# Two elements' WKV recurrence started earlier in the issue order of a fused Flamingo kernel: the third from the first place of the first grid batch, the fourth from its place 10

## The chip, the cores and the metric

One NeuronCore of one Trainium2 chip runs the whole program in one launch. The metric is the device time of that launch in microseconds (us). The kernel before was timed three times: 1096.87, 1093.98 and 1094.46, median 1094.46. A separate execution was profiled; its span, from the first instruction to the last, is 1092.4 us, and the launch around it took 1094.21.

Five instruction streams work side by side and meet at semaphores: PE (matmuls; its weight loads are listed as PEld), DVE (vector work, scans, reductions), ACT (activations and copies out of PSUM), POOL (a second, slower elementwise engine), and SP (issues the DMA transfers). Each stream runs its instructions in the order in which they were put there.

## What is computed

Four batch elements of 512 rows by 512 features go through two gated blocks, all in float32 at the interface:

```python
x = x + tanh(g_xattn[0]) * WKV(w, u, layernorm(x), ctx)        # a recurrence over the 512 rows
x = x + tanh(g_ffn[0])   * FFN(layernorm(x), w1, w2, w3)       # sign weights, activations rounded by groups of 64
x = x + tanh(g_xattn[1]) * ATT(layernorm(x), ctx, wq, wkv, wp) # 16 heads of 32, all 512 context rows
x = x + tanh(g_ffn[1])   * TERNARY(layernorm(x), gamma, W)     # one 512x512 layer, weights -1, 0, 1
```

The recurrence of the first line, per feature, for each row t with k = layernorm(x) and v = ctx:

```python
no = max(o, u + k);  A = exp(o - no);  E = exp(u + k - no);  y = (A*p + E*v) / (A*q + E)
no2 = max(w + o, k); A2 = exp(w + o - no2); E2 = exp(k - no2)
p, q, o = A2*p + E2*v, A2*q + E2, no2
```

The elements do not depend on each other. Within one element the four lines depend on each other in this order, so the WKV of an element has to be through before its FFN begins.

## The kernel before

**How a WKV is tiled.** `wkv_layer` handles one element. It takes the statistics of the four row tiles of 128 (L191, L194 on DVE), centres each tile (L215 on ACT), turns it on PE (`wk_ps`, four 128x128 transposes for a tile) and copies it out (L584 on ACT), so that features lie on partitions and the 512 rows lie along the free axis. Then come four chunks of 128 features. A chunk is a chain across engines: a scan for the running maximum (L599, DVE), a subtraction (L608, POOL), four activations and two exponentials (L612, L614, ACT), a scan for q (L629, DVE), products (L630 POOL, L632 DVE), a scan for p (L634, DVE), sums and products (L635, L636, L641, L642, POOL), two reciprocals of 256 columns (L640, DVE), the last product (L645, DVE), four transposes back (`wy_ps`, PE) and the gated sum into x (L653, DVE). For the third and fourth element a chunk also loads its v from a scratch tensor in HBM (L594, `wk_v<-cD`, issued by SP). The pool of these tiles has one buffer of each name, so that two chunks overlap only at their ends. The four chunks follow each other eight steps apart (`in_steps(chains, 8)`), 32 steps in all.

**How the order of the work is set.** The stages of all elements are Python generators. Each is registered with `line(...)` and a list of parts `(start, end, steps)`, which give every step a place on one axis; `run` always advances the generator whose next step has the lowest place. The places decide in which order the stages' matmuls stand in PE's queue, because each step's matmuls are tied behind those of the step before. The streams of the other engines are filled from the same sequence, with some reordering by the scheduler of the framework.

The axis: 0 to 0.3 is the start (context keys and values, weights, WKV of the first element). From 0.3 to 0.97 the FFN of the first element runs, 16 units of one row tile and one block of 512 hidden features each (`at_unit(n)` is its unit n). Then come three grid batches, from place b to b + 1 for b = 1, 2, 3. Each has 17 slots (`SLOTS`), and a slot is 1/17. In grid batch b the FFN of element b takes its 16 units, one in a slot, and between them stand the steps of the attention of element b - 1 (from slot 5 on, over 18 slots, so that it reaches slot 6 of the next batch), then the output projection of that element (`project_out`, slots 6 to 8 of the next batch) and its ternary layer (`ternary`). After the third batch the attention of the fourth element runs alone.

**Where the four WKVs stood.** The first element's is in the start. The second's is in the first FFN, its 32 chunk steps from unit 5 to unit 14. The third's and the fourth's were placed by one loop, `for b in (2, 3)`: x is loaded 4.2 slots before place b - 1, the statistics are taken 3.2 slots before it, the four transposing steps are at its slots 1.8 to 5.8, the 32 chunk steps at its slots 5.05 to 13.05. So the first grid batch had the whole WKV of the third element, the second grid batch that of the fourth, and the third grid batch had none.

**Names that the steps below touch.** `ff_hp` and `ff_acc` (L162) are the matmuls of the FFN, `tp_ps` (L165) the transposes between them. A unit's chain from the second `ff_hp` group runs over L750, L222, L676, L678, L680 (DVE), L684 (ACT), L685 (POOL) to `tp_ps`. `s_ps`, `pt_ps`, `o_ps` are the matmuls of the attention, L948 and L950 its maximum and exponential, L970 the copy of the turned scores. `at_o`, `qr_ps` and `p_ps` belong to the output projection; `tf_xn`, `qr_ps` and `f_ps` belong to the ternary layer, whose chain to PE is L219 and L1147 (POOL), L222 to L1159 (DVE), L231 (ACT). L724 loads FFN weights, L913 the attention's keys and queries.

Of the kernel before, what the change touches and what calls it, by code (L numbers as in the profile page):

```python
# [30 lines left out]
def kernel(  # L31
# [518 lines left out]
    def load_batch(b):  # L550
        xb = st.tile([P, NT, D], F32, name=f"xb{b}", tag="xb")
        rows = x[b].rearrange("(t p) d -> p t d", p=P)
        if b:
            nc.sync.dma_start(out=xb, in_=rows)
        else:
            for t in range(NT):
                nc.sync.dma_start(out=xb[:, t, :], in_=rows[:, t, :])
        return xb
# [628 lines left out]
    def next_batch(b):  # L1187
        xs[b] = load_batch(b)
        yield
        yield from wkv_layer(b, xs[b])  # L1190
# [15 lines left out]
    def run(until):  # L1206
        while lines:
            now = min(lines, key=place)
            if place(now) > until:
                return  # L1210
            try:
                next(now["gen"])
                now["step"] += 1
                next_turn()
            except StopIteration:
                lines.remove(now)
# [3 lines left out]
    SLOTS = NT * NF + 1  # L1220

    def line(gen, *parts, aside=False):
        lines.append({"gen": gen, "parts": parts, "step": 0, "aside": aside})

    xs = {}
    with (
# [19 lines left out]
        def at_unit(n):  # L1246
            return 0.3 + 0.67 * n / 16.0
# [84 lines left out]
            (at_unit(16), at_unit(16.4), 7),  # L1332
        )
        line(next_batch(1), (at_unit(0.5), at_unit(0.5), 1), (at_unit(0.6), at_unit(0.6), 1), (at_unit(2.0), at_unit(5.0), 4), (at_unit(5.0), at_unit(14.0), 32))
        for b in (2, 3):
            line(
                next_batch(b),
                (b - 1.0 - 4.2 / SLOTS, b - 1.0 - 4.2 / SLOTS, 1),
                (b - 1.0 - 3.2 / SLOTS, b - 1.0 - 3.2 / SLOTS, 1),
                (b - 1.0 + 1.8 / SLOTS, b - 1.0 + 5.8 / SLOTS, 4),  # L1340
                (b - 1.0 + 5.05 / SLOTS, b - 1.0 + 13.05 / SLOTS, 32),
            )
        run(0.99)
    nc.sync.dma_start(out=gamma_b, in_=bcast(gamma))
    ps = ctx.enter_context(tc.tile_pool(name="ps", bufs=1, space=PSUM))
# [78 lines left out]
```

## Time and profile before

| | us |
|---|---|
| median of three runs | 1094.46 |
| the profiled execution, launch and span | 1094.21, 1092.4 |
| PE busy in the span | 943.3 |
| DVE busy | 827.0 |
| ACT busy | 729.9 |
| POOL busy | 320.7 |

Busy time is summed over one engine's instructions, overlaps counted once. Matmuls have modelled ends, so a PE that is shown busy may still run at half its clock; the profile has a column for the clock that was granted (1.00 is full). The grid batches can be found in the trace by the matmuls of their FFNs: the first `ff_hp` matmul of the second element starts at 329 us, that of the third at 513, that of the fourth at 738, and the third batch's 16 slots are over at about 925. So the three batches took 184, 225 and 187 us.

### The profile page before, as it was taken

To read this page: it belongs to the slowest core of one execution; us is meant where nothing else is said; L and a number is where in the kernel's file an instruction comes from. 1 tells how busy PE (TensorE), PEld (TensorE's weight loads), DVE (VectorE), ACT (ScalarE), POOL (GpSimd) and SP (SyncE) were. 2 spreads that over 40 slices of the span, in tenths; PEclk is the share of its full clock that TensorE was granted. 3 is DMA by queue.
4 is the path that set the end of the run, shared out by engine and by line. 5 is a ranking of instruction groups with operands and counts; after the bars stand their busy time and mean duration, and the time that the engine had idled before them with its cause. 6 is when DMAs were issued, how large, how long until landed. Compare 5 with 4: busy or idle time off the path is not lost.

```text
span 1092.4 us, 17928 instructions
## 1 busy us (share of the span) xinstructions
PE 943.3 (86%) x6350; PEld 680.0 (62%) x6380; DVE 827.0 (76%) x1600; ACT 729.9 (67%) x1490; POOL 320.7 (29%) x328
## 2 busy tenths in 40 slices
PE   3879997998879888799997886999999999878975
PEld 2345564565557666677775665677776777655652
DVE  5985548757876899896769898966687866579976
ACT  5656755567545776667877576677685777877863
POOL 3831104423333254621215545412122410100000
PEclk8889999999999999999999798999999999989998
DMA  8188845464445674645576354655574563244311
GB/s 288 39 272 317 323 169 190 144 221 155 154 146 181 221 234 127 231 129 169 185 234 204 121 177 133 204 195 180 184 231 156 184 210 116 59 148 116 116 42 39
DMA packets 85674, 189.68 MB, mean 174 GB/s; under 512 B 12241, under 2 KB 36817, under 8 KB 74577
## 3 DMA queue, kind: packets, MB, share of 16 engines
q1 hardware_dynamic: 85584, 188.53, 51.7%
q8 instruction: 51, 0.84, 0.3%
q14 instruction: 39, 0.31, 0.1%
HBM read 148.65 MB, written 39.85 MB: 173 GB/s over the span
## 4 chain that ended last, share of the span: by engine, by line
PE 49%; DVE 22%; ACT 14%; POOL 5%; issue 5%; DMA 4%; SPq 1%; ACTq 0%; POOLq 0%; DVEq 0%
PE ff_hp L162 15%; PE pt_ps L165 7%; PE ff_acc L162 6%; PE o_ps L162 4%; PE v_ps L162 4%; PE s_ps L162 3%; ACT at_P L950 3%; DVE wk_q L640 3%; ACT at_PT L970 3%; DVE at_nm L948 2%; PE k_ps L162 2%; DVE wk_p L634 1%; PE qr_ps L165 1%; PE tp_ps L165 1%; ACT wk_e L612 1%
## 5 line engine op out<-in xcount | busy, mean ns | idle before, releaser
L162 PE MATMUL ff_hp<-wT,xp 128*128 128x512 f32 x1024 | 275.7, 412 | 6.6 <-DVE ff_z L746 3.7
L162 PEld LDWEIGHTS ff_hp<-wT,xp 128*128 128x128 f32 x1024 | 195.4, 196 | 54.6 <-DVE ff_z L746 5.7
L950 ACT ACTIVATE at_P<-s_ps,at_nm 128x512 f32<-128x512 f32 x256 | 175.0, 690 | 45.2 <-DVE at_nm L948 43.4
L948 DVE TENSOR_REDUCE at_nm<-s_ps 128x1 f32<-128x512 f32 x256 | 166.6, 677 | 38.4 <-PE s_ps L162 37.9
L970 ACT COPY at_PT<-pt_ps 128x512 f32<-128x512 f32 x224 | 131.2, 590 | 72.6 <-PE pt_ps L165 71.9
L685 POOL TENSOR_TENSOR ff_z<-qg_b,qg_s 128x512 f32<-128x512 bf16 x64 | 71.9, 1124 | 314.6 <-ACT qg_b L684 304.7
L165 PE MATMUL pt_ps<-ident,at_P 128*128 128x128 f32 x1024 | 155.4, 280 | 9.0 <-ACT at_PT L970 4.3
L165 PEld LDWEIGHTS pt_ps<-ident,at_P 128*128 128x128 f32 x1024 | 118.1, 142 | 47.3 <-ACT at_PT L970 10.9
L162 PE MATMUL ff_acc<-wT,hr 128*128 128x512 f32 x512 | 137.6, 409 | 5.2 <-DVE hr L697 2.6
L162 PE MATMUL s_ps<-at_kR,at_qR 128*128 128x512 f32 x256 | 103.0, 464 | 24.0 <-ACT at_P L950 17.6
L162 PEld LDWEIGHTS ff_acc<-wT,hr 128*128 128x128 f32 x512 | 92.9, 191 | 26.2 <-DVE hr L697 4.2
L162 PE MATMUL o_ps<-at_PT,at_V 128*32 128x128 f32 x2048 | 75.4, 281 | 4.7 <-ACT at_PT L970 2.8
L162 PEld LDWEIGHTS o_ps<-at_PT,at_V 128*32 128x32 f32 x2048 | 54.8, 111 | 28.6 <-issue 11.6
L746 DVE SCALAR_TENSOR_TENSOR ff_z<-ff_z,ff_hp 128x512 f32<-128x512 f32 x64 | 43.4, 679 | 37.0 <-ACT ff_z L745 36.9
L745 ACT ACTIVATE ff_z<-ff_hp,coef 128x512 f32<-128x512 f32 x64 | 44.1, 688 | 40.5 <-PE ff_hp L162 38.1
L750 DVE SCALAR_TENSOR_TENSOR ff_z<-ff_hp,coef,ff_z 128x512 f32<-128x512 f32 x64 | 47.7, 745 | 30.2 <-PE ff_hp L162 30.1
L684 ACT CAST qg_b<-qg_i 128x512 bf16<-128x512 int8 x80 | 49.3, 617 | 27.4 <-DVE qg_i L680 17.3
L162 PEld LDWEIGHTS s_ps<-at_kR,at_qR 128*128 128x128 f32 x256 | 43.3, 194 | 36.4 <-ACT at_P L950 25.2
L162 PE MATMUL v_ps<-wkvT,cT 128*128 128x512 f32 x128 | 60.5, 618 | 5.5 <-DVE wT L303 2.3
L162 PE MATMUL k_ps<-cT,wkvT 128*128 128x512 f32 x128 | 61.3, 631 | 2.3 <-ACT wk_k L584 1.0
L640 DVE RECIPROCAL wk_q<-wk_q 128x256 f32<-128x256 f32 x32 | 54.5, 1722 | 3.0 <-POOL wk_q L635 1.6
L696 ACT CAST hr<-tp_ps 128x512 fp32r<-128x512 f32 x64 | 37.6, 588 | 21.7 <-PE tp_ps L165 21.7
(180 smaller groups left out, 1669.4 us busy)
## 6 DMA issues: line engine op xcount, KB each, us to landing
wT<-wD SPq DMA_DIRECT2D x72, 1024.0 KB, 5.4
wn<-in_L_ffn_w_dram SPq DMA_DIRECT2D x18, 1024.0 KB, 6.2
at_kR<-kD SPq DMA_DIRECT2D x128, 128.0 KB, 4.0
at_qR<-qD SPq DMA_DIRECT2D x256, 64.0 KB, 2.5
wD<-wT SPq DMA_DIRECT2D x12, 1024.0 KB, 4.2
kD<-k_half SPq DMA_DIRECT2D x16, 512.0 KB, 2.8
qD<-at_half SPq DMA_DIRECT2D x32, 256.0 KB, 2.2
cn<-in_ctx_dram SPq DMA_DIRECT2D x8, 512.0 KB, 5.9
```

The lines of the kernel that those rows point to most:

```text
L162: return in_turn(nc.tensor.matmul(*args, **kwargs))
L165: return in_turn(nc.tensor.transpose(*args))
L640: nc.vector.reciprocal(half, half)
L684: nc.scalar.copy(qb, qi)
L685: nc.gpsimd.tensor_tensor(grouped(src), grouped(qb), s.unsqueeze(2).to_broadcast([P, NG, GS]), ALU.mult)
L696: nc.scalar.copy(part[:, 0, :], pt)
L745: nc.scalar.activation(z, hp, AF.Tanh, scale=coef[:, 0:1])
L746: nc.vector.scalar_tensor_tensor(z, z, 1.0, hp, ALU.add, ALU.mult)
L750: nc.vector.scalar_tensor_tensor(z, hp, coef[:, 1:2], z, ALU.mult, ALU.mult)
L948: nc.vector.tensor_reduce(nm, sp, AX.X, ALU.max, negate=True)
L950: nc.scalar.activation(lanes[k, i, t], sp, AF.Exp, bias=nm, accum_out=sums[k][:, t, i : i + 1],)
L970: made[k] = nc.scalar.copy(dst, blocks(pt))
```

## The change

The loop over the third and fourth element is replaced by two calls, one for each, with other places. Nothing is computed in another way, and no instruction is added or removed.

```diff
-        for b in (2, 3):
-            line(
-                next_batch(b),
-                (b - 1.0 - 4.2 / SLOTS, b - 1.0 - 4.2 / SLOTS, 1),
-                (b - 1.0 - 3.2 / SLOTS, b - 1.0 - 3.2 / SLOTS, 1),
-                (b - 1.0 + 1.8 / SLOTS, b - 1.0 + 5.8 / SLOTS, 4),
-                (b - 1.0 + 5.05 / SLOTS, b - 1.0 + 13.05 / SLOTS, 32),
-            )
+        line(
+            next_batch(2),
+            (at_unit(12.0), at_unit(12.0), 1),
+            (at_unit(13.6), at_unit(13.6), 1),
+            (at_unit(14.2), at_unit(16.2), 4),
+            (1.0 + 1.0 / SLOTS, 1.0 + 9.8 / SLOTS, 32),
+        )
+        line(
+            next_batch(3),
+            (1.0 + 5.0 / SLOTS, 1.0 + 5.0 / SLOTS, 1),
+            (1.0 + 7.5 / SLOTS, 1.0 + 7.5 / SLOTS, 1),
+            (1.0 + 9.8 / SLOTS, 1.0 + 11.8 / SLOTS, 4),
+            (1.0 + 12.0 / SLOTS, 2.0 + 7.0 / SLOTS, 32),
+        )
```

For the third element the transposing steps move into units 14.2 to 16.2 of the first FFN, and the chunks start at slot 1 of the first grid batch, 2.2 slots for each chunk where there were 2. For the fourth element the statistics move to slot 7.5 of the first grid batch, the transposing steps to slots 9.8 to 11.8, and the four chunks stand at slots 12, 15, 18 and 21 counted from place 1, three slots for each. So two of its chunks are in the first grid batch, and two are in the first seven slots of the second. The WKV of the first and second element stay where they were.

## The prediction

> **What bounds the kernel now.** I read the sums by stretch first: the three grid batches, cut where the first `ff_hp` matmul of each FFN starts in the timeline (329, 513, 738 us) and where the 16 slots of the third are over (925).
>
> ```profile
> 329.00:513.00 184.00, 163.34 (x1087) 126.95 (x1089) 157.15 (x284) 125.50 (x261) 70.94 (x71) 0.96 0.56 182
> 513.00:738.00 225.00, 196.51 (x1437) 151.22 (x1444) 181.49 (x358) 158.89 (x332) 85.96 (x82) 0.95 0.55 183
> 738.00:925.00 187.00, 181.40 (x1392) 141.67 (x1399) 134.36 (x304) 132.52 (x293) 44.02 (x44) 0.99 0.56 179
> ```
>
> Columns: length, then busy time of PE, PEld, DVE, ACT, POOL, the granted clock, DMA share, GB/s. The third batch, without a WKV, is bound by PE (181.4 of 187). The second has the same FFN, attention, projection and ternary work and a WKV on top: 47.1 us more DVE, 15 us more PE, and 38 us more time. The excess is what can be won.
>
> Then the same by sub-stretch, cut at slots 5, 10, 12 of the first batch and slot 7 of the others.
>
> ```profile
> 329.00:376.00 47.00, 42.94 (x204) 32.89 (x205) 33.00 (x61) 27.33 (x50) 11.91 (x13) 0.97 0.62 202
> 376.00:428.00 52.00, 44.34 (x306) 34.51 (x308) 50.97 (x81) 38.89 (x83) 23.95 (x24) 0.97 0.56 182
> 428.00:454.00 26.00, 23.33 (x170) 18.18 (x168) 23.30 (x42) 17.78 (x39) 16.38 (x17) 0.93 0.65 211
> 454.00:513.00 59.00, 52.72 (x413) 41.37 (x411) 49.88 (x106) 41.49 (x92) 18.70 (x17) 0.97 0.47 153
> 513.00:593.00 80.00, 74.33 (x554) 57.58 (x556) 59.86 (x120) 61.20 (x131) 24.02 (x23) 1.00 0.62 210
> 593.00:738.00 145.00, 122.18 (x884) 93.64 (x889) 121.63 (x239) 97.68 (x203) 61.94 (x60) 0.92 0.51 168
> 738.00:810.00 72.00, 70.99 (x540) 55.96 (x543) 53.02 (x120) 53.69 (x119) 14.03 (x15) 1.00 0.60 194
> 810.00:925.00 115.00, 110.41 (x854) 85.71 (x857) 81.34 (x185) 78.84 (x175) 29.99 (x30) 0.99 0.53 170
> ```
>
> Call them A to H. B is DVE-bound (51.0 of 52); A has 14 us of free DVE. F is bound by neither engine and lasts 30 us longer than H, its twin without a WKV; its clock is 0.92. So I asked what PE waited for in F:
>
> ```profile
> PE qr_ps L165 <- ACT tf_xn L231: 8.6, 1, 8.6
> PE qr_ps L165 <- ACT at_o L231: 3.9, 1, 3.9
> PE tp_ps L165 <- DVE at_y L1036: 2.7, 1, 2.7
> PE f_ps L162 <- ACT at_PT L970: 2.2, 1, 2.2
> ```
>
> In H no such wait is above 0.9 us. These are the projection's and ternary layer's chains, arriving late. The chain of waits around the longest of them shows why:
>
> ```profile
> 644.59 1.59 POOL wk_e L630
> 646.18 1.45 POOL ff_z L685
> 647.63 2.17 POOL wk_q L635
> 649.86 1.63 issue
> 651.49 1.70 DVE wk_q L640
> ...
> 663.13 1.52 POOL tf_xn L219 x2
> 664.64 0.50 POOL tf_xn L1147
> ```
>
> WKV work on POOL and DVE stands directly ahead of the rest.
>
> **The change part by part.** No instruction is added; work moves. One chunk costs DVE, from the mean rows of L599, L629, L632, L634, L640 (twice), L645, L653: 1.41 + 1.34 + 1.01 + 1.84 + 3.44 + 0.97 + 0.74 = 10.75 us. Its slowest rows (2.22, 2.23, 1.78, 2.29, 3.50, 1.73, 0.75) give 14.5, the upper bound of a chunk; 3.7 us more. ACT has four 0.72 and two 1.07, 5.0; POOL six operations, 1.42 + 1.56 + 1.44 + 1.7 + 1.36 + 1.29 = 8.8; PE four transposes of 0.27. I take DVE as the measure, because it was full where chunks ran, and B's fullness (0.98) as the pace of a full stretch.
>
> *A, slots 0 to 5.* The third element's chunks now start at slot 1. Out: its early scans, 2.5 us in the timeline. In: two chunks and one scan, 22.9. DVE: 33.0 - 2.5 + 22.9 = 53.4, at 0.98 it is 54.5: +7.5. PE work (43) cannot hide it. Bounds: +6.4 (DVE wholly full) to +14 (two chunks at 14.5). A chunk's own chain is no tighter: the gated sums came at 396.1, 420.2, 446.4 and 473.0 us, 24 to 27 us apart, and A would give 27 for each. PE's order has the first `wy_ps` transposes in slot 3 and the next in slot 5; if a chain is late there, PE stands, with `ff_acc` and the second `ff_hp` queued behind. That is inside the 7.5.
>
> *B, slots 5 to 10.* WKV in B was 22.6 us of DVE; now chunks three and four less the scan, 20.1, and the fourth element's statistics, 4 x 0.85 = 3.4. DVE 51.9, at 0.98 53: +1 (0 to +3).
>
> *C, slots 10 to 12.* A gap. DVE loses 8.3, PE loses one `wy_ps` group and gets the fourth element's 16 `wk_ps` transposes, 16 x 0.32 = 5: 27.2, less the 1.7 that a half-clock stretch in it (0.93) cost. Bound by PE: 0 (0 to +2).
>
> *D, slots 12 on.* Out: 9.3 of WKV and 3.4 of statistics; in: nearly two chunks, 20. DVE 49.9 - 12.7 + 20 = 57.2, PE 52.7 unchanged. At 0.96 for both 59.6, and I take 61, since both are nearly full: +2 (0 to +5.5).
>
> *E, slots 0 to 7 of the second batch.* Out: 11.6 of WKV on DVE, 16 `wk_ps`. In: two chunks and a remainder of 1.7, 23.2. DVE 71.5, PE 74.3 - 5.1 + 3.3 = 72.5. Its twin G lasts 72. Two engines at 0.94 give 77: -3 (-8, G's length, to +4, DVE at 78.8).
>
> *F.* No WKV is left in it: H's 115, and 2 for the remaining disorder: 117, -28. Bounds -30 (H) to -13 (the 17.4 us of waits above stay, and only the rest goes).
>
> *The first FFN's end.* Twelve `wk_ps` transposes and three centrings and copies move into it: 3.8 us of PE, in the stretch from 300 to 329 us, where PE was busy 23.0 of 29. The idle 6 us hide them; where they don't, it is 3.8. I take +1 (0 to 3.8). The x load keeps its place in SP's queue in both built programs.
>
> *SP.* A v load (L594) waits for the chunk before it (L636 on POOL), and what follows in the queue waits with it: now FFN weights (L724) and the first q stores in A, later queries (L913).
>
> ```profile
> SPq L594 <- POOL wk_e L636: 28.2, 6, 8.3
> ```
>
> These were prefetched by a slot or more, so I take +2 (0 to 8, one longest wait uncovered).
>
> Sum: 7.5 + 1 + 0 + 2 - 3 - 28 + 1 + 2 = -17.5. On the profiled span, 1092.4 - 17.5 = 1074.9. The median is 2.06 above that span (1094.46 - 1092.4), so 1077.
>
> **A rule that speaks against it.** DVE's L632 takes 0.68 us at best and 1.78 at worst, with POOL reading at the same time. The Trainium skill, page "SBUF — State Buffer", section "SBUF: two separate sides", says that a DVE operation with two SBUF inputs and a POOL operation that reads SBUF exclude each other for a whole instruction. A holds the attention's POOL work, and now WKV's too. By the rule each of a chunk's five such operations could wait for a POOL operation of 1.27 us, on top of the shortest rows' 9.0: 15.4 for a chunk, and A would be +16 instead of +7.5. The mean rows contain such encounters already, so the sum goes by them.
>
> **The rivals.** (1) *The first batch swallows it.* DVE's free time in A and D takes the chunks, E runs at G's pace: all the low bounds together, 6.4 - 8 - 30 = -31.6, 1063. For: A and D have 14 and 9 us free. Against: a chunk is a serial chain over four engines with single buffers. (2) *Work only changes place.* A chunk costs 9.5 us (38/4) wherever it is; six in the first batch, two in the second: 1094. For: DVE is 0.85 full in the first batch already. Against: slots 5 to 13, first `ff_hp` to first `ff_hp` (366 to 469 us), took 12.9 us each, the two after 480 some 11: 3.8 for a two-slot chunk, far below 9.5. (3) *Slower: the waits in F are the ternary layer's own.* If POOL, DVE and ACT deliver `tf_xn` and `at_o` as late without WKV, the 17.4 us and the half-clock stretches around them stay (598 to 605, 615 to 622, 656 to 667, some 8 us of loss beside the waits): F gains 5, E 3, and 13.5 are paid elsewhere: +5.5, 1100. It decides from F gaining less than 10. For: the operation that ends each wait is the layer's own. Against: H has the same chains without such waits.
>
> **How the numbers follow.** Forecast 0.70, rival 1 0.10, rival 2 0.08, rival 3 0.12. The forecast's own range is 1064 to 1090. A measurement can tell 0.3% from no change (1091.2 to 1097.7). Faster: forecast less 0.01, rival 1 and a quarter of rival 2, 0.81; same: half of rival 2 and 0.02 from the edges of the forecast and rival 3, 0.06; slower 0.13. All high bounds together (1121) are no case; 1063 to 1092 leaves out rival 3, most of rival 2 and a tail below, 0.2.
>
> **What would show it.** The second batch from first `ff_hp` to first `ff_hp` near 197 us, its PE waits on `tf_xn` and `at_o` under 1 us each and the clock near 1.0 after slot 7; the first batch near 194, with DVE above 0.95 in slots 0 to 10; the third at 187. Wrong would be a first batch above 212, `wy_ps` waits in slots 3 and 5 above a few us, or F above 132 us.

## The result

The changed kernel took 1105.77 us in the median of four runs (1102.51 to 1107.30), the kernel before 1094.39 on the same chip (1093.98 to 1096.87). The ratio is 1.0095, its 95% interval 1.0068 to 1.0122. I had forecast 1077 within 1063 to 1092: the sign was wrong. The profiled execution of the changed kernel took 1107.30, its span is 1105.5.

The sums by stretch, cut as before at the first `ff_hp` of each FFN (columns: length, busy time of PE, PEld, DVE, ACT, POOL, granted clock, DMA share, GB/s):

```profile
333.00:540.00 207.00, 172.03 (x1095) 132.19 (x1098) 176.03 (x297) 134.51 (x274) 89.68 (x89) 0.92 0.53 169
540.00:752.00 212.00, 192.53 (x1417) 149.08 (x1424) 166.43 (x346) 146.82 (x313) 69.53 (x66) 0.95 0.54 179
752.00:939.00 187.00, 181.17 (x1400) 141.25 (x1410) 135.34 (x306) 133.90 (x296) 44.02 (x44) 1.00 0.59 192
```

The second batch won 13 us, the first lost 23, the third is as it was, and the first batch starts 4 us later. DVE's sum in the first batch, 176 us, is close to what the prediction's parts add up to (157 + 20); but the stretch lasted 207 us, far longer than that sum. The sub-stretches A to F of the prediction, cut at the same units of the FFN in both kernels (A holds the first six units, so it ends where slot 6 begins; B holds four, C two, D four, E seven, F nine):

```profile
333.00:394.00 61.00, 46.62 (x201) 34.88 (x204) 54.20 (x76) 32.93 (x58) 31.48 (x32) 0.92 0.54 174
394.00:453.00 59.00, 50.22 (x308) 38.09 (x307) 49.48 (x86) 36.12 (x77) 23.81 (x23) 0.86 0.48 154
453.00:475.00 22.00, 21.87 (x178) 17.93 (x177) 20.33 (x53) 18.94 (x42) 8.24 (x10) 1.00 0.65 216
475.00:540.00 65.00, 53.32 (x414) 41.30 (x412) 52.02 (x86) 46.52 (x100) 26.15 (x24) 0.97 0.52 163
540.00:632.00 92.00, 79.03 (x546) 61.16 (x549) 77.82 (x144) 63.96 (x133) 34.84 (x33) 0.91 0.54 181
632.00:752.00 120.00, 113.50 (x873) 87.92 (x876) 88.61 (x203) 82.85 (x181) 34.70 (x34) 0.99 0.54 178
```

| | before | forecast | measured |
|---|---|---|---|
| A, slots 0 to 5 | 47 | 54.5 | 61 |
| B, slots 5 to 10 | 52 | 53 | 59 |
| C, slots 10 to 12 | 26 | 26 | 22 |
| D, slots 12 on | 59 | 61 | 65 |
| E, slots 0 to 7 of the second batch | 80 | 77 | 92 |
| F, the rest of the second batch | 145 | 117 | 120 |

F came nearly as forecast. The reader should look at E: DVE is busy 77.8 of 92 us and PE 79.0, so neither engine is full, and the stretch is still 20 us longer than its twin without a WKV (72). The granted clock is 0.91 in E and 0.86 in B. Lost clock costs PE at most (1 - clock) x length: 8 us in each.

The waits of PE in A, and those in E, say what stood in the way (engine, line, what it waited for: us, times, longest):

```profile
PE wy_ps L165 <- DVE wk_e L645: 4.1, 1, 4.1
PE tp_ps L165 <- POOL ff_z L685: 3.1, 1, 3.1
PE ff_hp L162 <- DVE ff_z L750: 2.5, 1, 2.5
```

```profile
PE qr_ps L165 <- ACT at_o L231: 4.2, 1, 4.2
PE ff_hp L162 <- DVE ff_z L746: 3.5, 1, 3.5
PE s_ps L162 <- ACT at_P L950: 3.1, 2, 2.8
PE ff_hp L162 <- DVE ff_z L750: 2.6, 1, 2.6
```

Two pieces of the timeline show how such a wait comes about (start, length, instruction, in brackets the engine's own idle time before it and what ended it). The first is in A, the second in E, with the ACT instruction that L746 needs:

```profile
352.48 1.43 DVE L632 TENSOR_TENSOR wk_q<-wk_e,wk_q 128x512 f32<-128x512 f32 x1
353.84 1.22 DVE L634 TENSOR_TENSOR_SCAN wk_p<-wk_e 128x512 f32<-128x512 f32 x1
356.16 3.37 DVE L640 RECIPROCAL wk_q<-wk_q 128x256 f32<-128x256 f32 x2 [1.11 <-POOL wk_q L635]
359.44 0.65 DVE L750 SCALAR_TENSOR_TENSOR ff_z<-ff_hp,coef,ff_z 128x512 f32<-128x512 f32 x1
360.10 1.73 DVE L645 TENSOR_TENSOR wk_e<-wk_e,wk_q 128x512 f32<-128x512 f32 x1
```

```profile
565.71 0.69 ACT L745 ACTIVATE ff_z<-ff_hp,coef 128x512 f32<-128x512 f32 x1
568.53 2.27 DVE L634 TENSOR_TENSOR_SCAN wk_p<-wk_e 128x512 f32<-128x512 f32 x1 [1.17 <-POOL wk_e L630]
570.73 0.66 DVE L746 SCALAR_TENSOR_TENSOR ff_z<-ff_z,ff_hp 128x512 f32<-128x512 f32 x1
```

In A, DVE works 7 us for the chunk, 1.1 of it standing idle for POOL, before it takes the 0.65 us of L750 that the FFN's unit needs; PE, whose order has `wy_ps` next, stands 4.1 us until L645 is done: here it waits for the chunk itself. In E it waits for FFN work behind the chunk: L746's input is done at 566.4, but the scan L634 stands before it in DVE's queue, first waits 1.17 us for POOL, then takes 2.27 us, and L746 starts at 570.7: PE's 3.5 us. A queue that runs in order can be the bound without being full.

### The profile page after: what moved, and what is told of

It reads as the page before. It is cut to its first block, busy times and chain, and to the rows that moved or that the text cites. A ratio compares the mean times of both kernels' runs of the same rounds, so it can differ in the third digit from the quotient of the medians.

```text
span 1105.5 us, 17930 instructions
## 1 busy us (share of the span) xinstructions
PE 948.9 (86%) x6350; PEld 683.9 (62%) x6380; DVE 832.4 (75%) x1600; ACT 731.7 (66%) x1490; POOL 322.2 (29%) x328
## 4 chain that ended last, share of the span: by engine, by line
PE 49%; DVE 25%; ACT 12%; POOL 6%; issue 5%; DMA 3%; SPq 0%; POOLq 0%; ACTq 0%; DVEq 0%
PE ff_hp L162 16%; PE pt_ps L165 7%; PE ff_acc L162 6%; PE o_ps L162 4%; PE s_ps L162 3%; PE v_ps L162 3%; ACT at_P L950 3%; PE k_ps L162 3%; DVE wk_q L640 2%; ACT at_PT L970 2%; DVE wk_p L634 2%; DVE at_nm L948 2%; PE qr_ps L165 2%; DVE qg_i L680 2%; DVE ff_z L750 1%
## 5 line engine op out<-in xcount | busy, mean ns | idle before, releaser
L162 PE MATMUL ff_hp<-wT,xp 128*128 128x512 f32 x1024 | 281.9, 419 | 18.4 <-DVE ff_z L746 8.3
L162 PEld LDWEIGHTS ff_hp<-wT,xp 128*128 128x128 f32 x1024 | 198.9, 199 | 70.1 <-DVE ff_z L746 11.7
L685 POOL TENSOR_TENSOR ff_z<-qg_b,qg_s 128x512 f32<-128x512 bf16 x64 | 72.0, 1125 | 318.9 <-ACT qg_b L684 305.4
L750 DVE SCALAR_TENSOR_TENSOR ff_z<-ff_hp,coef,ff_z 128x512 f32<-128x512 f32 x64 | 47.4, 741 | 32.8 <-PE ff_hp L162 32.7
L746 DVE SCALAR_TENSOR_TENSOR ff_z<-ff_z,ff_hp 128x512 f32<-128x512 f32 x64 | 43.4, 679 | 36.7 <-ACT ff_z L745 36.5
L697 DVE TENSOR_TENSOR hr<-tp_ps,hr 128x512 fp32r<-128x512 f32 x64 | 43.7, 682 | 12.1 <-ACT hr L696 12.0
```

The lines of the kernel that those rows point to most:

```text
L162: return in_turn(nc.tensor.matmul(*args, **kwargs))
L685: nc.gpsimd.tensor_tensor(grouped(src), grouped(qb), s.unsqueeze(2).to_broadcast([P, NG, GS]), ALU.mult)
L697: nc.vector.tensor_tensor(part[:, 1, :], pt, part[:, 0, :].bitcast(F32), ALU.subtract)
L746: nc.vector.scalar_tensor_tensor(z, z, 1.0, hp, ALU.add, ALU.mult)
L750: nc.vector.scalar_tensor_tensor(z, hp, coef[:, 1:2], z, ALU.mult, ALU.mult)
```

## The experiments

Each run is set against executions of the kernel before on the same chip (medians 1093.98 to 1095.23); so the prices below are differences of ratios to it, times 1094.4. Stretch lengths are those of each run's own profile, cut at the same units.

**The third element alone** moved, the fourth at its old place (the diff is against the changed kernel, and the fourth's other three times go back in the same way):

```diff
-            (1.0 + 5.0 / SLOTS, 1.0 + 5.0 / SLOTS, 1),
+            (1.0 + 12.8 / SLOTS, 1.0 + 12.8 / SLOTS, 1),
...
```

> The third element's WKV at its new place (turned at the end of the first FFN, chunks from slot 1 to 9.8 of the first grid batch), the fourth's at its old one. Theory A (place): the first five slots, with FFN work alone, are a bad place, because a unit's chain there has only one slot of about 7 us and PE stands behind every late chain; so the first batch keeps most of its loss with four chunks instead of six: about 192 us (184 before, 207 in the changed kernel), the second batch 225 as before, the end of the first FFN +4, together 1104 to 1110. Rival B (number): six chunks in one batch are too much for DVE, four are not; first batch 180 to 186, second 225, together 1092 to 1098.

1098.96, ratio 1.0046 (1.0029 to 1.0064), between the two ranges and 1 us above Rival B's. A is 61 us, so Theory A's loss there is real; but C and D give it back (21 and 51), and the first batch sums to 186, as Rival B said. The kernel loses a few us at the end of the first FFN (its first batch starts at 333 instead of 329). Moving the third element alone makes the kernel 5 us slower; B, without the fourth's statistics, is 53.

**The fourth element alone** moved, behind the third at its old place (the fourth's lines):

```diff
+            (1.0 + 11.0 / SLOTS, 1.0 + 11.0 / SLOTS, 1),
+            (1.0 + 13.3 / SLOTS, 1.0 + 15.3 / SLOTS, 4),
+            (1.0 + 15.0 / SLOTS, 2.0 + 7.0 / SLOTS, 32),
```

> The third element's WKV at its old place (slots 5 to 13), the fourth's behind it: turned at slots 13.3 to 15.3, chunks from slot 15 of the first grid batch to slot 7 of the second, 2.25 slots each. Theory A: slots 0 to 12 of the first batch as before, the gain of 25 us after slot 7 of the second batch is kept, slots 0 to 7 of the second batch pay some 10 us for each of three chunks less what is there now (about 100 us against 80): 1085 to 1093. Rival B: with only one chunk more in the first batch and DVE not full in the second, slots 0 to 7 take no more than 80 and the kernel comes to 1068 to 1078.

1093.35, ratio 0.9986 (0.9972 to 0.9999), just above Theory A's range. F falls from 145 to 120; D rises from 59 to 72 and E from 80 to 90. What F gains, D and E pay. The two moves alone come to +5 and -2 us, both together to +10; but the fourth's places are not the same here and in the changed kernel, so the 7 us between are not shown to be crowding.

**What four chunks cost at each place.** Four runs left out an element's chunks in the kernel before and in the changed one:

```diff
+        if b in (3,):            # (2,) in the runs without the third element's
+            for _ in range(32):
+                yield
+            return
         chains = [chunk(c) for c in range(NC)]
```

> The kernel before with the four chunks of the fourth element's WKV left out (its statistics and transposes stay). It prices these chunks at their old place. Theory A and my forecast agree here: second batch near 190 us instead of 225, 1057 to 1064. Were the waits on the projection's and ternary layer's chains their own (rival 3 of the prediction), the second batch would stay above 205 and the kernel above 1072.

> The changed kernel with the same four chunks left out. Theory A: the first batch keeps a loss of some 10 us in its first ten slots (near 195), slots 0 to 7 of the second batch fall from 92 to 74, that is, two chunks cost about 9 us each there although DVE was busy only 77.8 of 92 us; 1070 to 1078 in all. Rival B (number): with four chunks the first batch falls to 184 or less, and the whole is 1057 to 1064, the same as the kernel before without these chunks. If slots 0 to 7 of the second batch stay above 85, the chunks there are not what made them long.

> The changed kernel with the four chunks of the third element's WKV left out (statistics and transposes stay). Theory P (a chunk has one price of 8 to 10 us, mostly PE waits and the half clock that follows them, wherever it stands): 1065 to 1073, slots 0 to 5 of the first batch near 44 us, slots 5 to 10 near 45. The model of my prediction (a stretch lasts as long as its fullest engine's sum) would give slots 0 to 5 at 44 and slots 5 to 10 at 47, and the whole 1068: the two differ in the next run, not here.

> The kernel before with the same four chunks left out: the price of the third element's chunks at their old place. Theory P: 31 to 39 us less, 1056 to 1064, first batch 146 to 152 us. The model of my prediction: PE-bound without them, 163 us of PE less 4.4 of transposes, that is some 162 with gaps, 22 us less, 1073. Far less than that, or far more, would mean that the place decides the price.

| left out | median, ratio and interval | price of the four chunks |
|---|---|---|
| fourth's, kernel before | 1060.70, 0.9688 (0.9672 to 0.9704) | 34 us |
| fourth's, changed kernel | 1066.07, 0.9738 (0.9721 to 0.9754) | 39 us |
| third's, kernel before | 1065.99, 0.9750 (0.9727 to 0.9773) | 27 us |
| third's, changed kernel | 1069.61, 0.9780 (0.9761 to 0.9798) | 35 us |

The prices are good to 2 or 2.5 us in the kernel before and 3.5 in the changed one. The fourth's chunks cost 34 us at their old place and 39 at the new one. Without them, E and F of the changed kernel are the first two lines here, and E and F of the kernel before the last two:

```profile
525.00:596.00 71.00, 70.24 (x539) 55.12 (x538) 51.72 (x117) 52.49 (x116) 13.73 (x14) 1.00 0.64 212
596.00:714.00 118.00, 112.54 (x876) 86.90 (x875) 89.31 (x210) 84.90 (x187) 34.64 (x34) 1.00 0.59 194
512.00:586.00 74.00, 72.62 (x556) 57.38 (x556) 52.58 (x118) 57.31 (x125) 13.71 (x14) 1.00 0.62 206
586.00:705.00 119.00, 112.81 (x877) 87.00 (x876) 89.26 (x210) 85.18 (x187) 34.63 (x34) 1.00 0.61 194
```

In the changed kernel E is 71 instead of 92 us: the fourth's chunk work in it, 26 us on DVE in the windows, made it 21 us longer in a stretch where DVE had 19 us free. Of the 21 us, 12 are PE standing (13.0 us of E with the chunks, 0.8 without) and 9 are PE busy longer (79.0 against 70.2) with nearly the same matmuls, at a clock of 0.91 instead of 1.00. So in E the price is PE's waits and the clock lost after them. The run as a whole (1066.07) lies between the ranges of Theory A and Rival B; A and B stay at 61 and 59 with four chunks in the first batch, so six were not needed to make them dear. In the kernel before without the fourth's chunks, the second batch takes 193 us instead of 225, and its waits of 8.6 us on `tf_xn` and 3.9 on `at_o` are gone (the longest left is 1.7): rival 3 of the prediction is refuted. The third's 27 us at the old place lie between the 22 of the prediction's model and the 31 that Theory P had as its least; its 35 at the new place are within Theory P's range, where the prediction's model gave the same time.

**Less DVE work in a chunk, or the same in two pieces**, both in the changed kernel:

```diff
             for h in range(2):
                 half = den[:, h * (T // 2) : (h + 1) * (T // 2)]
-                nc.vector.reciprocal(half, half)
+                if b < 2:                                  # first run
+                    nc.vector.reciprocal(half, half)
...
+                nc.vector.reciprocal(half, half)           # second run
+                if b and h == 0:
+                    yield True
```

> The changed kernel without the two reciprocals (3.44 of a chunk's 10.75 us on DVE) in the third and fourth elements' WKV. If the price is DVE time standing ahead of the FFN's and attention's short operations, it falls with it: eight chunks at some 3 us, 1077 to 1087. If the price is the number of links of the chunk's chain, or its work on ACT and POOL, it falls by less than 10 us: 1096 to 1104.

> The changed kernel with a chunk's two reciprocals in two steps instead of one (the spare step before the transposes back is used for it, so the number of steps stays): the same work, but other instructions may stand between the two halves in DVE's queue. If long uninterrupted DVE work is what PE waits for (waits of 2.5 to 4.8 us on ff_z and wk_e), these waits lose up to 1.7 us each and some of the half-clock stretches with them: 5 to 12 us less, 1094 to 1101. If only the sum of DVE work matters: 1103 to 1108.

The first run concerns the third and fourth element, the second the second element too. Without the reciprocals 1094.49, ratio 1.0000 (0.9990 to 1.0010): 27.5 us of DVE work less bring 10 us, between the ranges of the two expectations. In two steps 1096.81, ratio 1.0021 (1.0012 to 1.0030): 8 us for no work less, only some 2 us fewer. So the sum of DVE work is at most a part of what is paid for. The largest waits did not get shorter, though (4.9 and 3.5 us on L746, as in the changed kernel), so the expected mechanism, 1.7 us off each wait, is not what happened; L750 in A now goes between the halves, and B runs at a clock of 0.94 instead of 0.86, A at 0.84 instead of 0.92. Nor was there much to separate: in the changed kernel's trace, DVE already ran other instructions between the two reciprocals in seven of the eight chunks, and only the first chunk's pair stands together (the 3.37 us in A above). The edit also puts the second reciprocal, POOL's L641 and L642 and the last product one step later, so that the transposes back follow the product without a spare step. Which of these brings the 8 us is not shown.

**The statistics out of B:**

```diff
-            (1.0 + 7.5 / SLOTS, 1.0 + 7.5 / SLOTS, 1),
-            (1.0 + 9.8 / SLOTS, 1.0 + 11.8 / SLOTS, 4),
+            (1.0 + 10.4 / SLOTS, 1.0 + 10.4 / SLOTS, 1),
+            (1.0 + 11.0 / SLOTS, 1.0 + 12.4 / SLOTS, 4),
```

> The changed kernel with the fourth element's statistics moved from slot 7.5 to 10.4 of the first batch and its transposes to slots 11 to 12.4. Slots 5 to 10 took 59.0 us with these statistics (3.4 us of DVE) and 52.8 without them in the run with the third element alone. Theory (crowding): in a stretch where DVE is full, 3.4 us more make PE wait a little and then run at half clock (17 us of it there); moved out, slots 5 to 10 fall to about 53 with less than 7 us at half clock, and the kernel to 1098 to 1102. If the statistics are not the cause, the stretch stays above 57 and the kernel within 3 us of the changed one.

B falls to 54 us as expected, but the kernel only to 1103.64, ratio 1.0076 (1.0061 to 1.0091): the other expectation, and not clear of the changed kernel's interval. A, whose program is the same, ran at a clock of 0.81 in this profile and 0.92 in that of the changed kernel:

```profile
331.00:393.00 62.00, 49.97 (x199) 38.26 (x201) 53.46 (x76) 32.23 (x57) 30.87 (x32) 0.81 0.50 166
393.00:447.00 54.00, 46.39 (x307) 35.49 (x307) 47.45 (x77) 35.45 (x76) 22.18 (x21) 0.94 0.51 169
```

A few us of a single stretch may be the clock of that execution. B also came to 53 to 56 us in four runs that leave the statistics where they were (without the reciprocals, with them in two steps, without Relu, without three POOL operations), so its 59 is not shown to be the statistics' doing.

**The split on the kernel before**, the same edit of the reciprocals:

> The kernel before with a chunk's two reciprocals in two steps instead of one. In the changed kernel this took 9 us away. If long uninterrupted DVE work is what makes a chunk dear, it does so at the old places too: 1084 to 1091. If it only mended the crowded slots of the changed kernel: 1092 to 1096.

1085.28, ratio 0.9910 (0.9891 to 0.9929), as the first theory had it: the fastest version with the whole computation, 10 us below the kernel before and 20 below the changed one. Here five of the eight pairs stood together before and one of eight with the edit; but the other moves that come with it are the same as above, so the separation alone is not shown to be the cause. F falls from 145 to 139, B and C by 3 together. In F the waits of 3.9 us on `at_o` and 2.7 on `at_y` are gone; the one on `tf_xn` stays, at 9.0.

**Work taken from a chunk on ACT and on POOL**, in the third and fourth element:

```diff
-                nc.scalar.activation(e[:, i, :], z, AF.Relu, bias=at, scale=sign)
+                if b < 2:        # without Relu: the exponentials read z, with scale 0
+                    nc.scalar.activation(e[:, i, :], z, AF.Relu, bias=at, scale=sign)
...
-            nc.gpsimd.tensor_tensor(E, E, v, ALU.mult)
-            nc.gpsimd.tensor_tensor(A, A, p[:, 0:T], ALU.mult)
-            nc.gpsimd.tensor_tensor(A, A, E, ALU.add)
```

> The changed kernel with the four Relu activations of a chunk (4 x 0.72 us on ACT) left out in the third and fourth elements' WKV, the exponentials reading z. 23 us of ACT work less, and the chunk's chain 2.9 us shorter; DVE's and POOL's work unchanged. If the chunk's price is the length of its chain or its share of ACT, 8 to 14 us less, like the 11 without the reciprocals: 1092 to 1098. If it is DVE's queue: 1102 to 1107.

> The changed kernel with three of a chunk's six POOL products and sums left out (L636, L641, L642, together 4.3 us) in the third and fourth elements' WKV. 35 us of POOL work less, the chain 2.7 us shorter. If the price is the chain or POOL standing ahead of the FFN's L685 (a wait of 3.1 us on it in slot 1), 8 to 14 us less: 1092 to 1098. If it is DVE's queue: 1102 to 1107.

> The kernel before with the four Relu activations left out in the third and fourth elements' WKV, as in the changed kernel, where 23 us of ACT work less made it 20.6 us faster. If ACT's queue sets a chunk's price at any place: 15 to 22 us less, 1073 to 1080. If only in the changed kernel's crowding: 1083 or more.

Without Relu, 23 us of ACT less: 20 us gained in the changed kernel (1085.19, ratio 0.9911, 0.9896 to 0.9925), more than expected, and 13 in the kernel before (1081.28, ratio 0.9885, 0.9870 to 0.9901), between the two expectations. Without the three POOL operations, 35 us of POOL less: 3 us (1102.29, ratio 1.0064, 1.0049 to 1.0079), in the range for DVE's queue, and not clear of the changed kernel's interval. So POOL's time is hardly paid for, as far as this run can tell.

The length of a chunk's chain is not settled by this pair, because the two runs do not shorten it alike, as the expectations took them to. Relu stands in front of the scan for q, where nothing runs beside it; L641 and L642 run beside the reciprocals, and from the start of L634 to the end of L645 the eight chunks together take 105 us with the three POOL operations and 103 without. From the start of L608 to the end of L645, waits for a step's turn included, they take 280 us in the changed kernel, 254 without Relu, 234 without the reciprocals, 296 without the POOL operations and 287 with the reciprocals in two steps; the gains are 20, 10, 3 and 8 us. So the gains do not follow the chain's length, but what Relu's 20 us owe to a shorter chain and what to ACT's queue is not separated. A stayed at 59 to 63 us in all of these runs of the changed kernel.

**Pace or place in A:** the third element alone, its chunks over slots 1 to 13.

```diff
-            (1.0 + 1.0 / SLOTS, 1.0 + 9.8 / SLOTS, 32),
+            (1.0 + 1.0 / SLOTS, 1.0 + 13.0 / SLOTS, 32),
```

> The third element's WKV alone moved, as in the run with the third element alone, but its chunks spread from slot 1 to 13 (three slots each) instead of 1 to 9.8. Slots 0 to 5 took 60.7 us there, and nothing taken from a chunk on DVE, ACT or POOL changed that. If it is the pace (a chunk's steps placed some 2 us apart in slots of 7 us, where each link takes 3, so that FFN operations queue behind steps that are not ready): slots 0 to 5 at 48 to 54 us, the kernel 1088 to 1095. If chunks in these slots are dear at any pace: 57 or more there, 1096 to 1101.

A is 59 us, so the place is dear at both paces tried; the kernel, 1093.73, ratio 1.0002 (0.9986 to 1.0018), comes out as the other theory had it, because B falls to 49. PE's waits in A are on L685 again:

```profile
PE tp_ps L165 <- POOL ff_z L685: 3.1, 1, 3.1
PE tp_ps L165 <- POOL ff_xn L685: 2.7, 2, 2.3
PE ff_hp L162 <- DVE ff_z L746: 2.1, 1, 2.1
```

**Relu shared out over other engines,** the computation whole, on top of the split. Two of four go to POOL, later to DVE:

```diff
+                if b and sign > 0:
+                    nc.gpsimd.tensor_scalar(e[:, i, :], z, at, 0.0, ALU.add, ALU.max)  # nc.vector later
+                else:
                     nc.scalar.activation(e[:, i, :], z, AF.Relu, bias=at, scale=sign)
```

> The kernel before with the reciprocals in two steps and, for all elements but the first, the two Relu activations of positive sign taken from ACT to POOL (add and maximum in one operation, some 0.77 us like L219 there). 1.4 us of a chunk's 5.0 on ACT less. If a microsecond of ACT work in a chunk costs most of a microsecond of the kernel (20.6 us for 23 in the run without Relu) and one of POOL a tenth (3.5 for 35), eight chunks give 8 to 11 us beyond the split's: 1073 to 1079. If ACT mattered only in the changed kernel: 1083 to 1087.

> The changed kernel with the same two edits as the kernel before in this set (reciprocals in two steps, two of four Relu on POOL). If the order of the places is worth what it was: some 10 us above that kernel, 1084 to 1090. If the new places were only bad because a chunk was dear on ACT, the two come within 4 us of each other.

> The kernel before with the reciprocals in two steps and, for all elements but the first, the two Relu activations of positive sign taken from ACT to DVE (add and maximum in one operation; the nearest row, L421, took 0.4 us). On POOL the same operation took 2.0 to 2.3 us and cost 23 us, so that run said nothing of ACT. If ACT's queue is the dearer part of a chunk (0.57 us of the kernel for each us of Relu left out at the old places, against 0.41 for each us of reciprocal): eight chunks in the grid batches at -0.8 + 0.3 us, 3 to 6 us below the run with the split alone, 1078 to 1083. If DVE's queue is: 1086 to 1092.

> The same two edits on the layout of the run with the fourth element alone (third at its old place, fourth from slot 15 of the first batch to slot 7 of the second). That layout was 1 us off the kernel before. If a chunk's price is the same at both places also when it is cheaper: within 4 us of the other run of this set. If the cheaper chunk fits into slots 0 to 7 of the second batch, where neither DVE nor ACT was full: 5 to 12 us below it.

All four missed the times expected. On POOL: 1108.55, ratio 1.0135 (1.0118 to 1.0152) at the old places and 1108.72, ratio 1.0133 (1.0109 to 1.0157) at the new. One such operation took 2.0 us, not 0.77:

```profile
L613 POOL TENSOR_SCALAR wk_e<-wk_p,uc x12: 1992/1996/2961, 167.5 to 682.4; 128x512 f32<-128x512 f32 x12
```

So each chunk has 4 us of POOL work more, and the two layouts come out alike, within the 4 us of the second theory; but with a dearer chunk on POOL that says nothing of ACT. On DVE, at 0.48 us: 1092.39, ratio 0.9986 (0.9973 to 0.9998), 8 us worse than the split alone, most of it in the first FFN, whose second element's WKV was changed too (its first batch starts at 335 instead of 328 us); the two batches together are 3 us longer. With the fourth element's layout 1101.36, ratio 1.0058 (1.0039 to 1.0078).

## Why the prediction was wrong

- *What bounds the kernel.* The reading of F held: its excess over H was the WKV's, and it fell by 25 us of the 28 forecast. Rival 3 was wrong, as the run without the fourth's chunks shows. What undid F's gain is in A, B, D and E.
- *The step that failed* is "I take DVE as the measure, ... and B's fullness (0.98) as the pace of a full stretch": each stretch was given its fullest engine's sum, at 0.94 to 0.98. By that rule E was to last 77 us; it lasted 92 with DVE 0.85 and PE 0.86 full. In E, a chunk's price was not its sum on the fullest engine but the waits that it puts before PE and the clock lost after them (12 and 9 of 21 us), and these came in slots with free DVE time as well.
- *Rival 2 came nearest in kind,* and was not right either (that rival 3's 1100 was nearer in number was luck: it had F gaining 5). "A chunk costs 9.5 us wherever it is": measured 7 to 8.5 us at the old places and 9 to 10 at the new ones, so work was not swallowed, but the new places are dearer by 13 us in all, and the kernel lost 10 where rival 2 had none. My argument against it, 3.8 us for a two-slot chunk, does not stand: the two units after 480 us did not take "some 11" us but 14 and 19 (first `ff_hp` at 480.5, 494.5, 513.4), and the run without the third's chunks puts a chunk in those slots at 7.
- *A* was +14, the upper bound, not +7.5; two chunks of 14.5 us are not what happened, since DVE's sum there was 54.2 us, near the 53.4 worked out. I had weighed the late `wy_ps` in slot 3 and called it "inside the 7.5"; it alone stood 4.1 us. Neither ACT's nor DVE's nor POOL's share of a chunk explains A, nor does the pace; what remains is that the slots with FFN work alone, about 7 us long, leave no room for a late unit's chain. That is argued, from waits on L685, L746 and L750, and not shown; the cause in A stays open.
- *The rest:* B +7 instead of +1, at a clock of 0.86 (with the statistics moved out it was +2, but so it was in runs that left them in); E +12 instead of -3; D +6 instead of +2; the first FFN's end +4 instead of +1. C gained 4 that I had not counted: only twelve of the sixteen `wk_ps` transposes fell into it, and four of them take PE some 0.6 us together, not 4 x 0.32. The +2 for SP's queue did not come: PE's waits on a DMA are 1.0 us from 300 to 752 us, 0.6 before.
- *The clock* was in the sum only as a gain in C. From 0.96 to 0.92 in the first batch is at most some 9 of the 23 us that it lost.
- *The Trainium skill's rule* of the shared SBUF port ("SBUF — State Buffer", "SBUF: two separate sides") bears on E's scan, and the trace agrees with it: in E, POOL's L635 started first and took 1.25 us, and L634 beside it took 2.27; in A, L634 started first and took 1.22, and L635 took 2.07. By the rule A was to cost +16 and it cost +14; but the run without three POOL operations left A at 59, so these, at least, are not its cause.
- *Open:* which engine's queue, or how much the chain's length, carries the price. Leaving out Relu on ACT gave 0.55 to 0.9 us for each us left out, reciprocals 0.4, POOL 0.1; yet moving half the Relu to DVE did not help.

## What to carry to other kernels

Price a block of work by leaving it out at both places before moving it; here that would have shown 61 us for eight chunks against 74. A stretch in which no engine is full need not have free time, since its engines run in order: ask which instruction stands behind each moved one, and whether the moved one's input is ready by then. Putting the two reciprocals into two steps, with the work behind them one step later, brought 8 to 10 us, where moving the whole block lost 10; which part of that edit does it is open.

## What the runs showed of the hardware

- In the changed kernel's first two batches, nine of eleven half-clock stretches set in within some 2 us of the end of a PE wait of 2.2 to 4.8 us. Their length varies between executions of the same instructions: after a wait of 2.5 us on L750 in A it was 3.4 us in the changed kernel's profile and 10.2 in that of the run with the statistics moved; A ran at 0.92, 0.89 and 0.81 in three profiles.
- On POOL, add and maximum with a per-partition scalar took 2.0 us for 128x512 float32, where multiply and add (L219) takes 0.77; on DVE it took 0.48.
